# Recurrent scans over 32 images: statistics and row loads on ScalarE, the last drain in quarters

## The chip, the cores and the metric

The kernel runs on one core of a Trainium2 chip. The metric is the device time of one execution in microseconds (us). The engines are TensorE (PE; its weight loads are PEld), VectorE (DVE), ScalarE (ACT), GpSimd (POOL) and SyncE (SP). SP and ACT each own a queue from which transfers are issued.

## The reference

The input x has 32 images of 48 channels, 64 rows and 128 columns in float32. Two layers are alike: `x = x + scans(group_norm(x))`. The group norm uses 16 groups of 3 channels per image. Cut to what matters, one layer's scans are:

```python
def step(w, b):                       # 1-d convolution over 5 taps, 48 -> 48 channels
    return lambda carry, inp: inp + conv1d(carry, w, b)
D = scan(step(down_w, down_b), rows 0..63 of x)       # along a row, from row to row
U = scan(step(down_w, down_b), rows 63..0 of D)       # the end rows as D has them
R = scan(step(right_w, right_b), columns 0..127 of U) # along a column
L = scan(step(left_w, left_b), columns 127..0 of R)
```

Each step needs the one before it: 63 + 63 row steps and 127 + 127 column steps per layer and image.

## The kernel before, in words

A pass takes 8 images through one layer, so there are 8 passes: 0 to 3 for the four groups of images in layer 0, 4 to 7 in layer 1. (In names of the profile `row_12u` is layer 1, group 2, up: pass 6.) A pass has four stages:

- down and up: one `row_step` per row, nine matmuls (L323) with block weights `wd`, and three VectorE operations (L331) that add bias and input. The rows lie in the tile `arena` (view `rows`, 384 elements per row).
- `hand_over`: while up runs, finished rows are moved within `arena` to the layout for columns (view `cols`, which begins where row 20 ends). Twenty transfers (two row parities, ten pieces of channels) move 8 rows; the column steps need them all, column e of a row of eight needs the pieces of e.
- right and left: one `col_step` per column in two halves, six matmuls (L345 to L349) and two VectorE operations (L352).

Beside the stages runs side work, each a Python generator that the driving loop at the end of the program advances at chosen steps:

- `prepare` of the next group, in right: load x (L233, two transfers per tile of 4 rows), bn_stats on VectorE (L177), transpose on POOL (L243), store to the DRAM stage `xin` (L246).
- `drain` of the pass before, in down and up: `residual` loads the layer's input again (L283) and adds it on POOL. In layer 0 the sum goes into `arena` in place (L286), is stored to `mid`, and bn_stats on VectorE collect it for layer 1. In layer 1 it goes to the tile `perm` (L298) and out (L305). `cols` and `rows` share memory, so a row can be loaded for the next pass only when the chunks over it are drained.
- `fetch` loads rows from `xin` or `mid` (L257, nine or ten transfers per 8 rows on SP's queue) and normalises them in place with 24 ScalarE operations (L261). The first 20 rows are fetched in left, the others behind the chunks that free them.

After the last pass, its drain stands alone. At the start, group 0's preparation stands alone.

Instructions of an engine run in a written order, made from the program order by a scheduler of the framework. Semaphores order the engines. All transfers, of SP's and ACT's queue together, take eight completion semaphores (DMAHW0 to DMAHW7) in turn in the scheduled order, and a transfer waits for the one before it on its semaphore. A transfer behind a waiting one on its queue waits too.

Of the kernel before, what the change touches and what calls it, by code (L numbers as in the profile page):

```python
# [30 lines left out]
F32 = mybir.dt.float32  # L31
# [24 lines left out]
EARLY = 3  # L56

# [27 lines left out]
def kernel(  # L85
# [40 lines left out]
    maskp = const([P, NG, FULL], "maskp")  # L126
    last = const([FULL, ROW], "last")
# [13 lines left out]
    nc.gpsimd.memset(arena[32:64], 0.0)  # L141
    for t in nats + perms:
        nc.vector.memset(t[32:64], 0.0)
    nc.vector.memset(wd, 0.0)
    nc.scalar.dma_start(mask_sb, mask)
# [25 lines left out]
    def stat_tile(n, name, key):  # L171
        return stat_pool.tile([P, n], F32, tag=name, name=f"{name}_{key}")

    def collect(st, j: int, t, key: str):

        for b in range(GB):
            nc.vector.bn_stats(st[:, b, j, :], t[:, b])  # L177

    def scaling(st, key: str):

        mv = stat_tile(2 * GB, "mv", key).rearrange("p (b k) -> p b k", k=2)
        for b in range(GB):
            nc.vector.bn_aggr(mv[:, b], st[:, b].rearrange("p j k -> p (j k)"))
        ps = ps_stat.tile([FULL, NG + 1, 2 * GB], F32, tag="ps_stat", name=f"ps_{key}")
        nc.tensor.matmul(ps[0:P, NG, 0:GB], mask_sb, mv[:, :, 0], start=True, stop=True)
        pair = stat_tile(2 * GB, "pair", key)
        nc.vector.tensor_copy(pair[:, 0:GB], mv[:, :, 0])
        dev = stat_tile(GB, "dev", key)
        nc.vector.tensor_tensor(dev, mv[:, :, 0], ps[0:P, NG, 0:GB], ALU.subtract)
        sq = stat_tile(GB, "sq", key)  # L190
        nc.vector.tensor_tensor(sq, dev, dev, ALU.mult)
        nc.vector.tensor_tensor(pair[:, GB:], sq, mv[:, :, 1], ALU.add)
# [29 lines left out]

    def prepare(g: int):


        st = stat_pool.tile([P, GB, NCH, 6], F32, tag="st", name=f"st_x{g}", bufs=1)
        for j in range(NCH):
            nat, perm = nats[j % 2], perms[j % 2]
            h0 = 2 * CH * j
# [9 lines left out]
            collect(st, j, nat, f"x{g}_{j}")  # L239
# [10 lines left out]
        return scaling(st, f"x{g}")  # L250

    def fetch(layer: int, g: int, j: int, scale, offset):
# [3 lines left out]
        for e, c0, c1, o, p0 in PIECES:  # L256
            nc.sync.dma_start(rows[p0 : p0 + c1 - c0, hs, o], src[e][c0:c1])  # L257
# [11 lines left out]
    def hand_over(j: int):  # L269

        qs = slice(RB // 2 * j, RB // 2 * (j + 1))
        for r in range(2):
            src = rows[:, RB * j : RB * (j + 1)].rearrange("p (q r) o n -> r o p q n", r=2)
            dst = cols[SIDES[r], qs].rearrange("p q e k b -> e p q (k b)")
            for e, c0, c1, o, p0 in PIECES:
                nc.sync.dma_start(dst[e][c0:c1], src[r, o][p0 : p0 + c1 - c0])
# [84 lines left out]
    def drive(gen, key):  # L361

        coeffs[key] = yield from gen
# [126 lines left out]
```

## Time and profile before

| what | us |
|---|---|
| runs | 6104.42, 6104.59, 6112.84; median 6104.59 |
| profiled execution | 6102.24 |
| its span, first to last instruction | 6100.3 |
| granted TensorE clock | 0.919 of full speed |
| start, until the first row step | 182.5 |
| down / up / right / left, shortest seen | 136.7 / 127.2 / 172.7 / 170.2 |
| last drain, behind the last column step | 212.6 |

An engine's busy time is the sum of its instructions' durations. "Idle before" is how long it stood before instructions of a group, with what ended the wait. Stages are read by windows of time: the length of a window, what each engine was busy in it, and the clock that TensorE was granted.

### The profile page before, as it was taken

The numbers are of one execution on the slowest core, as the hardware profiler recorded it, in microseconds if no ns is written. First come the engines' busy times: TensorE is split into PE (matmuls) and PEld (weight loads), VectorE is DVE, ScalarE is ACT, GpSimd is POOL, SyncE is SP. The second block draws the span as 40 slices with busy tenths as digits, with TensorE's granted clock in tenths as the row PEclk, the third lists the DMA queues.
The fourth block names the chain that finished last, engine by engine and source line by source line (L and its number), as shares of the span: only waits on it lengthen the run. The fifth ranks groups of instructions, "written<-read, shape, count | busy, mean of one in ns | idle before, by whom it ended". The sixth has DMA issues, their size and how long they took to land. (4 is left out here: it accounts for less than half of the span.)

```text
span 6100.3 us, 102555 instructions
## 1 busy us (share of the span) xinstructions
PE 5016.6 (82%) x42592; PEld 4979.0 (82%) x42592; DVE 2870.0 (47%) x8277; ACT 843.3 (14%) x1737; POOL 1067.5 (17%) x333
## 2 busy tenths in 40 slices
PE   0799987889878898689987999779988699796960
PEld 0799987889878898689977999779988699796960
DVE  3446555555555555545555455334543255343530
ACT  0600222002220021202031200302022200400000
POOL 5103012120120201200022001420034000430025
PEclk9999998999989999899988999889999799898985
DMA  6636246552464533632065401642045500642014
GB/s 141 134 90 137 42 85 132 118 119 46 85 133 112 118 53 76 136 85 40 1 121 126 89 1 37 130 112 55 1 83 123 127 1 1 131 116 58 1 43 112
DMA packets 646130, 511.64 MB, mean 84 GB/s; under 512 B 55616, under 2 KB 596288, under 8 KB 645664
## 3 DMA queue, kind: packets, MB, share of 16 engines
q1 hardware_dynamic: 639680, 504.18, 38.6%
q8 instruction: 335, 5.49, 0.4%
q10 hardware_dynamic: 5984, 0.90, 0.1%
q14 instruction: 131, 1.07, 0.1%
HBM read 253.23 MB, written 150.99 MB: 66 GB/s over the span
## 5 line engine op out<-in xcount | busy, mean ns | idle before, releaser
L298 POOL TENSOR_TENSOR perm<-arena,nat 112x1024 f32<-112x1024 f32 x128 | 486.8, 3832 | 2304.1 <-DVE arena L352 1809.3
L261 ACT ACTIVATE arena<-arena,offset_m,scale_m 128x128 f32<-128x128 f32 (+1 forms) x864 | 420.6, 584 | 2203.6 <-DMA arena<-mid 1298.0
L286 POOL TENSOR_TENSOR arena<-arena,nat 112x2048 f32<-112x2048 f32 x64 | 288.7, 4529 | 1635.8 <-DVE arena L352 1072.6
L261 ACT ACTIVATE arena<-arena,offset_x,scale_x 128x128 f32<-128x128 f32 (+1 forms) x864 | 419.6, 583 | 771.9 <-DMA arena<-xin 730.6
L243 POOL COPY perm<-nat 112x1024 f32<-112x1024 f32 x128 | 254.3, 2021 | 904.6 <-DMA nat<-in_x 683.3
L177 DVE BATCH_NORM_STATS2 st_m<-arena 112x6 f32<-112x256 f32 x512 | 273.7, 605 | 17.7 <-POOL arena L286 17.7
L177 DVE BATCH_NORM_STATS2 st_x<-nat 112x6 f32<-112x256 f32 x512 | 179.7, 411 | 116.7 <-DMA nat<-in_x 113.8
L323 PE MATMUL row_10d<-arena,wd 128*128 128x128 f32 x1134 | 149.6, 300 | 44.4 <-DVE arena L331 39.1
L323 PE MATMUL row_02d<-arena,wd 128*128 128x128 f32 x1134 | 149.9, 300 | 44.0 <-DVE arena L331 38.9
L323 PE MATMUL row_03d<-arena,wd 128*128 128x128 f32 x1134 | 146.4, 295 | 47.4 <-DVE arena L331 43.8
L323 PEld LDWEIGHTS row_10d<-arena,wd 128*128 128x128 f32 x1134 | 146.2, 214 | 47.6 <-DVE arena L331 42.0
L323 PEld LDWEIGHTS row_02d<-arena,wd 128*128 128x128 f32 x1134 | 146.6, 215 | 47.2 <-DVE arena L331 41.8
L323 PE MATMUL row_01d<-arena,wd 128*128 128x128 f32 x1134 | 150.2, 301 | 41.8 <-DVE arena L331 37.6
L323 PEld LDWEIGHTS row_03d<-arena,wd 128*128 128x128 f32 x1134 | 142.4, 209 | 51.2 <-DVE arena L331 42.8
L323 PEld LDWEIGHTS row_01d<-arena,wd 128*128 128x128 f32 x1134 | 146.8, 215 | 45.0 <-DVE arena L331 40.5
L323 PE MATMUL row_11d<-arena,wd 128*128 128x128 f32 x1134 | 140.9, 290 | 39.5 <-DVE arena L331 39.5
L323 PE MATMUL row_12d<-arena,wd 128*128 128x128 f32 x1134 | 139.9, 289 | 39.9 <-DVE arena L331 28.2
L323 PEld LDWEIGHTS row_11d<-arena,wd 128*128 128x128 f32 x1134 | 138.4, 205 | 41.9 <-DVE arena L331 41.8
L323 PEld LDWEIGHTS row_12d<-arena,wd 128*128 128x128 f32 x1134 | 137.5, 204 | 42.2 <-DVE arena L331 42.2
L323 PE MATMUL row_13d<-arena,wd 128*128 128x128 f32 x1134 | 137.4, 286 | 40.3 <-DVE arena L331 28.1
L323 PEld LDWEIGHTS row_13d<-arena,wd 128*128 128x128 f32 x1134 | 135.1, 201 | 42.6 <-DVE arena L331 42.6
L323 PE MATMUL row_02u<-arena,wd 128*128 128x128 f32 x1134 | 143.3, 294 | 17.2 <-DVE arena L331 17.2
(199 smaller groups left out, 13052.8 us busy)
## 6 DMA issues: line engine op xcount, KB each, us to landing
arena<-arena SPq DMA_DIRECT2D x768, 96.0 KB, 2.3
nat<-in_x SPq DMA_DIRECT2D x128, 384.0 KB, 6.4
xin<-perm SPq DMA_DIRECT2D x128, 384.0 KB, 4.8
nat<-xin SPq DMA_DIRECT2D x128, 384.0 KB, 8.3
mid<-arena SPq DMA_DIRECT2D x128, 384.0 KB, 5.1
nat<-mid SPq DMA_DIRECT2D x128, 384.0 KB, 6.3
out<-perm SPq DMA_DIRECT2D x256, 192.0 KB, 2.7
arena<-xin SPq DMA_DIRECT2D x168, 192.0 KB, 5.6
```

The source lines that it names most:

```text
L177: nc.vector.bn_stats(st[:, b, j, :], t[:, b])
L243: nc.gpsimd.tensor_copy(perm5[:, r], nat[:, r])
L261: nc.scalar.activation(view[:, o, b], view[:, o, b], AF.Identity, bias=offset[:, o, b : b + 1], scale=scale[:, o, b : b + 1],)
L286: nc.gpsimd.tensor_tensor(res, res, nat, ALU.add)
L298: nc.gpsimd.tensor_tensor(perm[:, t].rearrange("p (b k e) -> p b k e", b=GB, k=NK), cols[:, q + t].rearrange("p e k b -> p b k e"), nat[:, ...
L323: nc.tensor.matmul(ps[o][:, a:b], wd[:, n], prev[:, i, a + s * GB : b + s * GB], start=seen[o] == 1, stop=seen[o] == left[o],)
```

## The change

The change has six parts.

1. Row loads of `fetch` are issued on ACT's queue (L352 in the changed program), just ahead of the 24 ScalarE operations that use them.
2. bn_stats on VectorE stay for group 0 alone. For the other groups `input_moments` loads x a second time in 16 halves of images, and `result_moments` loads `mid` again in 16 tiles. `collect` sums each tile on ScalarE with an accumulator (L195), POOL turns the sums into means (L199, L200), and a second ScalarE operation sums the squared deviations (L204). `scaling` joins the parts on VectorE.
3. In layer 0 the residual sum goes into the loaded tile `nat` (L382) instead of `arena`.
4. `drain` is advanced at every third step up to step 27. `input_moments` is advanced in down and up of the pass before the one it serves, `result_moments(0)` in those of pass 3, the others in right and left.
5. At the start, loads use free parts of `arena` as further staging tiles. The clear of `arena` is cut to 1536 elements and one clear per staging tile (L314), half of them on VectorE.
6. `hand_over` moves the last 8 rows in three parts (rows 4 to 7, 2 to 3, 0 to 1); their odd rows go on ACT's queue, 30 transfers per pass. The last pass is drained by `last_residual` in four parts of 32 columns, part 3 first, while left runs; part 0 stands behind the last step, with two thirds of its adds on VectorE and half of its stores on ACT's queue. The pieces in DRAM are 128 bytes.

```diff
-    nc.gpsimd.memset(arena[32:64], 0.0)
+    nc.gpsimd.memset(arena[32:64, H * ROW + 7 * CH * PAIR :], 0.0)
...
+    def collect(mo, t: int, views, key: str):
+        bs = slice(min(views), max(views) + 1)
+        for b, view in views.items():
+            nc.scalar.activation(
+                view, view, AF.Identity, scale=sides, accum_out=mo.mean[:, b, t : t + 1]
+            )
+        neg = stat_tile(GB, "neg", key)
+        nc.gpsimd.tensor_scalar(neg[:, bs], mo.mean[:, bs, t], -1.0 / mo.n, None, ALU.mult)
+        nc.gpsimd.tensor_scalar(
+            mo.mean[:, bs, t], mo.mean[:, bs, t], 1.0 / mo.n, None, ALU.mult
+        )
+        for b, view in views.items():
+            nc.scalar.activation(
+                view, view, AF.Square, bias=neg[:, b : b + 1],
+                accum_out=mo.dev2[:, b, t : t + 1],
+            )
...
+    def result_moments(g: int):
+        mo = Moments(NCH, W * CH, f"m{g}")
+        src = stages[1][g].rearrange("(q r) c n -> r c q n", r=2)
+        for j in range(NCH):
+            t = perms[j % 2]
+            for r in range(2):
+                nc.sync.dma_start(t[SIDES[r]], src[r, :, CH * j : CH * (j + 1)])
+            view = t.rearrange("p q (n b) -> p b (q n)", b=GB)
+            collect(mo, j, {b: view[:, b] for b in range(GB)}, f"m{g}_{j}")
+            yield
+        coeffs[1, g] = scaling(mo)
...
-            collect(st, j, nat, f"x{g}_{j}")
+            if first:
+                for b in range(GB):
+                    nc.vector.bn_stats(st[:, b, j, :], nat[:, b])
...
         for e, c0, c1, o, p0 in PIECES:
-            nc.sync.dma_start(rows[p0 : p0 + c1 - c0, hs, o], src[e][c0:c1])
+            nc.scalar.dma_start(rows[p0 : p0 + c1 - c0, hs, o], src[e][c0:c1])
...
-    def hand_over(j: int):
+    def hand_over(h0: int, h1: int):
         for r in range(2):
+            eng = nc.scalar if r and h1 <= RB else nc.sync
...
-                nc.sync.dma_start(dst[e][c0:c1], src[r, o][p0 : p0 + c1 - c0])
+                eng.dma_start(dst[e][c0:c1], src[r, o][p0 : p0 + c1 - c0])
...
-            nc.gpsimd.tensor_tensor(res, res, nat, ALU.add)
+            nc.gpsimd.tensor_tensor(nat, res, nat, ALU.add)
...
+    def last_residual(g: int, part: int):
+        kn = NK // 4
+        ks = slice(part * kn, (part + 1) * kn)
+        nq = 4 * CH
+        for i, q in enumerate(range(0, HP, nq)):
...
+            for t in range(nq):
+                for r in range(2):
+                    nc.sync.dma_start(nat[SIDES[r], t], ...)
+            for t in range(nq):
+                eng = nc.vector if part == 0 and t % 3 else nc.gpsimd
+                eng.tensor_tensor(perm[:, t], cols[:, q + t, :, ks], nat[:, t], ALU.add)
+                for r in range(2):
+                    dma = nc.scalar if part == 0 and r else nc.sync
+                    dma.dma_start(out[...], perm[SIDES[r], t])
+            yield
...
+            if h % RB == 0 and h:
+                hand_over(h, h + RB)
+            elif h in SPLITS:
+                hand_over(h, SPLITS[h])
...
+                if not nxt and i % 32 == 0:
+                    side["last"] = last_residual(g, i // 32)
+                if not nxt and i % 8 == 0:
+                    advance(side, "last")
```

(Views in `last_residual` are shortened here; `SPLITS = {4: 8, 2: 4, 0: 2}`.)

Three places show how the order of instructions moves. The first is POOL at the border from pass 0 to pass 1. Before, the transposes of x for group 1 are followed by the residual adds of pass 0's drain:

```order
L243 COPY perm_83<-nat_81 112x1024 x2
L243 COPY perm_82<-nat_80 112x1024 x2
L243 COPY perm_83<-nat_81 112x1024 x2
L286 ISA
L286 TENSOR_TENSOR arena<-arena,nat_80 112x2048
L286 TENSOR_TENSOR arena<-arena,nat_81 112x2048
```

After the change the means for group 2 (16 steps, two operations each, first and last shown) stand between the two:

```order
L331 COPY perm_84<-nat_82 112x1024 x2
L199 TENSOR_SCALAR neg_x_00_5779<-mean_x_5774 112x1
L200 TENSOR_SCALAR mean_x_5774<-mean_x_5774 112x1
...
L199 TENSOR_SCALAR neg_x_71_7844<-mean_x_5774 112x1
L200 TENSOR_SCALAR mean_x_5774<-mean_x_5774 112x1
L382 TENSOR_TENSOR nat_81<-arena,nat_81 112x2048
L382 TENSOR_TENSOR nat_82<-arena,nat_82 112x2048
```

ScalarE has the same there: its last sums for group 2 (L195, L204), then the row loads (L352) and their normalising operations (L356):

```order
L195 ACTIVATE perm_84,mean_x_5774<-perm_84,sides 112x2048
L204 ACTIVATE perm_84,dev_x_5775<-perm_84,neg_x_71_7844 112x2048
L352 DMA arena<-xin_86 48x8x128 x2
L352 DMA arena<-xin_86 32x8x128
L352 DMA arena<-xin_86 16x8x128
...
L356 ACTIVATE arena<-arena,offset_x_2744,scale_x_2742 128x8x16 x24
```

So the adds and the row loads of pass 1 stand behind all sums for group 2. The same holds in passes 2 and 3; in pass 3 it is 14 of the 16 sums of the first result.

The second place is the end of up in pass 1. Before, SP's last twenty pieces follow each other, each with the next semaphore:

```order
L276 DMA arena<-arena 48x4x128 [waits DMAHW5_49,DVE_49]
L276 DMA arena<-arena 48x4x128 [waits DMAHW6_49]
L276 DMA arena<-arena 32x4x128 [waits DMAHW7_49,PE_49]
L276 DMA arena<-arena 16x4x128 [waits DMAHW0_49,DVE_49]
L276 DMA arena<-arena 48x4x128 [waits DMAHW1_49]
```

After, these are SP's pieces of row 25 and its pairs (rows 25, 27, 29, 31) from the fourth on:

```order
L372 DMA arena<-arena 48x4x128 [waits DMAHW5_49]
L372 DMA arena<-arena 48x4x128 [waits DMAHW6_49]
L372 DMA arena<-arena 16x4x128 [waits DMAHW1_49]
L372 DMA arena<-arena 32x4x128 [waits DMAHW2_49]
L372 DMA arena<-arena 48x4x128 [waits DMAHW3_49]
```

and these are ACT's first pieces in that pass, of row 3 and of rows 5 and 7:

```order
L372 DMA arena<-arena 48x128 [waits DMAHW3_49,DMAHW2_49,DMAHW4_49,DVE_49,Activation_49]
L372 DMA arena<-arena 16x128 [waits DMAHW6_49,DMAHW5_49,Activation_49]
L372 DMA arena<-arena 32x128 [waits DMAHW7_49,DVE_49]
L372 DMA arena<-arena 32x2x128 [waits DMAHW2_49,DMAHW1_49,Activation_49]
```

In the scheduled order these stand among each other: SP's wait for DMAHW5 is for ACT's second piece here, those for DMAHW1 and DMAHW2 are for the pieces of rows 5 and 7. ACT's first piece waits for row 3 on VectorE (DVE). Behind the row-25 piece SP has 67 pieces up to and with the first of row 0.

The third place is the end of SP's queue. Before, the drain alternates loads of 4096-byte pieces and stores of 512-byte pieces:

```order
L283 DMA nat_80<-mid_91 48x2x1024
L305 DMA out<-perm_83 48x8x128 x4
L283 DMA nat_80<-mid_91 48x2x1024
L283 DMA nat_81<-mid_91 48x2x1024
L305 DMA out<-perm_82 48x8x128 x4
```

After, from the end of the last hand-over on:

```order
L416 DMA nat_81<-mid_92 48x8x32 x16
L416 DMA nat_82<-mid_92 48x8x32 x16
L432 DMA out<-perm_83 48x8x32 x16
L432 DMA out<-perm_84 48x8x32 x16
L416 DMA nat_81<-mid_92 48x8x32 x16
L432 DMA out<-perm_83 48x8x32 x16
```

Two chunks are loaded ahead; from the third on, 16 loads and 16 stores alternate, down to part 0, which has 8 stores per chunk on SP.

More of the change, by code (lines that the diff above doesn't have):

```diff
@@ L56 @@
 EARLY = 3
+SPLITS = {4: 8, 2: 4, 0: 2}
 PRODUCTS = (
@@ L171, in stat_tile @@
     def stat_tile(n, name, key):
[L172 to L183, printed above, removed]
+        bufs = 1 if n > 2 * GB else None
@@ L408 @@
     load_col_weights(0, nc.scalar)
-    for _ in drive(prepare(0), (0, 0)):
+    for _ in prepare(0):
         pass
```

195 lines of the change are left out of this document (148 added, 47 removed).

## The prediction

> **What bounds the kernel now.** I read the busy table first, then the busy time by stage, then the groups of instructions, and last the timeline of SP's queue at the places where TensorE stands still.
>
> ```profile
> span 6100.3 us, 102555 instructions
> PE 5016.6 (82%) x42592; PEld 4979.0 (82%) x42592; DVE 2870.0 (47%) x8277; ACT 843.3 (14%) x1737; POOL 1067.5 (17%) x333
> ```
>
> The recurrence on TensorE and VectorE is the bound, and it is 82% busy, so what can be won is where it waits. The windows are: the start, down and up of pass 0, the wait between up and right in pass 1, then down to the start of right for passes 1 to 4 and 5 to 7, the right stages of passes 0 to 3, the last left stage, the end. Behind the window stand its length, the engines' busy time, the granted clock, DMA share and GB/s.
>
> ```profile
> 0.00:182.50 182.50, 2.01 (x8) 1.81 (x8) 57.16 (x153) 4.81 (x11) 96.55 (x37) 1.00 0.66 148
> 182.50:319.20 136.70, 131.47 (x1135) 130.55 (x1136) 65.54 (x204) 101.23 (x208) 8.11 (x4) 1.00 0.64 116
> 319.20:446.40 127.20, 126.77 (x1136) 126.57 (x1134) 63.11 (x198) 0.00 (x0) 4.46 (x3) 1.00 0.38 92
> 1169.80:1178.30 8.50, 0.02 (x1) 0.05 (x1) 0.00 (x0) 0.00 (x0) 0.00 (x0) 0.70 0.49 120
> 814.10:1178.30 364.20, 289.61 (x2279) 284.87 (x2278) 192.25 (x527) 71.30 (x145) 72.69 (x17) 0.89 0.56 122
> 1575.60:1945.90 370.30, 294.30 (x2278) 289.55 (x2276) 192.60 (x527) 71.24 (x145) 72.59 (x17) 0.87 0.55 120
> 2345.20:2710.70 365.50, 285.50 (x2278) 280.15 (x2277) 192.20 (x527) 71.24 (x145) 72.61 (x17) 0.90 0.56 121
> 3053.70:3424.10 370.40, 293.73 (x2278) 288.97 (x2276) 192.61 (x527) 71.19 (x145) 72.63 (x17) 0.87 0.55 120
> 3767.10:4132.50 365.40, 267.47 (x2270) 264.91 (x2269) 122.61 (x379) 71.19 (x144) 123.58 (x33) 0.86 0.55 121
> 4474.60:4839.60 365.00, 266.55 (x2271) 264.03 (x2269) 122.44 (x379) 71.23 (x144) 123.40 (x33) 0.86 0.54 121
> 5183.00:5544.60 361.60, 264.06 (x2271) 261.61 (x2269) 122.35 (x379) 71.20 (x144) 123.55 (x33) 0.86 0.55 122
> 448.00:643.90 195.90, 180.27 (x1532) 177.51 (x1533) 124.97 (x377) 5.89 (x16) 51.99 (x26) 0.95 0.68 141
> 1178.30:1405.40 227.10, 194.19 (x1533) 191.08 (x1533) 132.82 (x401) 2.57 (x7) 63.81 (x32) 0.91 0.65 135
> 1945.90:2175.00 229.10, 195.92 (x1533) 192.84 (x1534) 132.78 (x401) 3.94 (x11) 63.85 (x32) 0.90 0.64 135
> 2710.70:2883.40 172.70, 172.68 (x1524) 172.70 (x1525) 88.72 (x253) 34.03 (x72) 0.00 (x0) 0.98 0.23 41
> 5716.90:5887.70 170.80, 170.41 (x1526) 170.21 (x1524) 89.43 (x255) 0.00 (x0) 0.00 (x0) 1.00 0.00 1
> 5887.70:6100.30 212.60, 0.00 (x0) 0.00 (x0) 0.00 (x0) 0.00 (x0) 117.75 (x32) 0.51 0.46 111
> ```
>
> Undisturbed, down takes 136.7, up 127.2, right 172.7, left 170.8. Right in passes 0 to 2 is 23, 54 and 56 longer, and VectorE is busy there for 36 to 44 us more. Down, up and the wait before right take 364 to 370 in passes 1 to 4 where pass 0 needs 265.5. The granted clock is 1.00 where nothing waits and 0.86 to 0.90 in the disturbed stretches; I let it come back with the waits gone. 395 us at the two ends have no recurrence at all.
>
> ```profile
> L177 DVE BATCH_NORM_STATS2 st_m<-arena 112x6 f32<-112x256 f32 x512 | 273.7, 605 | 17.7 <-POOL arena L286 17.7
> L177 DVE BATCH_NORM_STATS2 st_x<-nat 112x6 f32<-112x256 f32 x512 | 179.7, 411 | 116.7 <-DMA nat<-in_x 113.8 <-DMA maskp<-in_mask 2.8
> L261 ACT ACTIVATE arena<-arena,offset_x,scale_x 128x128 f32<-128x128 f32 x672 | 343.9, 608 | 717.0 <-DMA arena<-xin 687.0 <-DVE arena L331 30.0
> L261 ACT ACTIVATE arena<-arena,offset_x,scale_x 128x64 f32<-128x64 f32 x192 | 76.3, 494 | 54.9 <-DMA arena<-xin 43.6 <-DVE offset_x L220 11.3
> L298 POOL TENSOR_TENSOR perm<-arena,nat 112x1024 f32<-112x1024 f32 x128 | 486.8, 3832 | 2304.1 <-DVE arena L352 1809.3 <-DMA nat<-mid 354.4 <-issue 121.4
> ```
>
> **The statistics.** 896 of the 1024 bn_stats leave VectorE: per group 128 x 0.605 = 77 us in the down and up behind it, 128 x 0.411 = 53 us in right. In right nothing else is added, so passes 0 to 2 return to 172.5: 652.1 - 517.5 = **-135**. What replaces them is ScalarE's work on reloaded data. One normalising operation takes 343.9/672 = 0.51 us for 128 elements and 76.3/192 = 0.40 for 64, so by these two rows 0.28 and 1.8 ns per element: a 256-element sum is 0.74 and a result step of 16 such takes 12, an input step, two of 2048, at most 8. No row of this case shows an accumulator. With the hand to POOL and back I count 16 x 9 = 144 us for an input group and 16 x 12.5 = 200 for a result group. In the new order both stand ahead of the residual adds and the row loads on ScalarE, POOL and SP. They run in right and left, 342 us, behind the preparation of x, eight pairs of tiles at the pace of the start:
>
> ```profile
> 94.42 7.82 POOL L243 COPY perm<-nat 112x1024 f32<-112x1024 f32 x4 [9.86 <-DMA nat<-in_x]
> 111.68 7.81 POOL L243 COPY perm<-nat 112x1024 f32<-112x1024 f32 x4 [9.44 <-DMA nat<-in_x]
> ```
>
> 111.7 - 94.4 = 17.3 a pair, 140 in all, some 10 behind right's start. 150 + 144 = 294 is covered with 48 to spare. For the first result group, 150 + 200 = 350 is not quite, though its last two steps stand later: I put 10 us on pass 3, between 0 and 40. The reloads lie there too, and so does their traffic. Each group's scaling gains some ten small operations on VectorE, 0.4 us each at most by the row of L177; it is busy for 89 of 171 us in left, so I count nothing, and 8 x 4 = 32 if none were hidden.
>
> **Down and up, passes 1 to 4.** Row loads now need no turn on SP. A load is 9 or 10 issues on ScalarE's queue, about 6 us in which it computes nothing, some 2 to land, and 24 operations x 0.51 = 12.3: 20.5 us. Six stand behind each other from about 11 us on, so the rows from 60 on are ready at 134, where TensorE alone would be there at 60 x 2.17 = 130. The residual's sum goes to its own tile, so its rows are free at the add's end and not after store and bn_stats; that is in the 20.5 too. Down becomes 143 and up, free of bn_stats, 126.5. Between 136.7 and 160 is open.
>
> **The hand-over.** SP's issues in a row by the timeline (start, length, count), what one takes to land by the DMA table, and the spread of single issues (ns, least/median/most). T is the end of up, T0 the start of down.
>
> ```profile
> 4083.69 3.29 SPq L276 DMA_DIRECT2D arena<-arena  x5
> arena<-arena SPq DMA_DIRECT2D x768, 96.0 KB, 2.3
> arena<-mid SPq DMA_DIRECT2D x168, 192.0 KB, 5.1
> 4012.14 4.67 SPq L305 DMA_DIRECT2D out<-perm  x4
> 4026.31 4.66 SPq L305 DMA_DIRECT2D out<-perm  x4
> 3809.30 5.98 SPq L257 DMA_DIRECT2D arena<-mid  x9
> 3828.12 0.84 SPq L305 DMA_DIRECT2D out<-perm  x2
> L305 SPq DMA_DIRECT2D out<-perm x256: 315/392/1626, 3771.6 to 6096.5; - x128
> L257 SPq DMA_DIRECT2D arena<-mid x360: 302/450/1773, 2746.0 to 5345.1; - x180
> ```
>
> One piece costs 3.29/5 = 0.66 us of SP. Each transfer waits for the one eight before it in the common order, on whichever queue that is. Before, all were SP's, and with its 20 last pieces SP is past the end of up by 8.5. Now 30 odd-row pieces stand on ScalarE's queue, and the first of them waits for row 3, which is done three steps of 127.2/63 = 2.02 before the end of up, T - 6. But by the order SP's pieces of row 25 take the semaphore behind just these, so SP, whose rows 25 to 8 have long been finished, stands until T - 6 + 2.3 = T - 4. From there to the first piece of row 0 it issues 67 pieces: 67 x 0.66 = 44, which lands at **T + 42**. In passes 3 and 4 row loads stand among them, and three that SP waits for take 5.1 - 2.3 = 2.8 more: T + 50; in pass 0 reloads of x do the like, and I take 50 too. Without this coupling, SP has 50 left at the end and right starts at about T + 10. Passes 1 and 2: 143 + 126.5 + 42.5 = 312 against 364.2 and 370.3, -52 and -58; pass 3 321 + 10 = 331, -34; pass 4 321, -49: together **-193**. Pass 0 loses: 137 + 127 + 50, with 3 for issues between the normalising steps, 317 against 265.5, **+51**.
>
> **Passes 5 to 7.** What is late here is SP itself: the chunks' stores come 4026.3 - 4012.1 = 14.2 apart where no row load stands between; where one does, it takes about 6 us of SP. Before, the last ended at 4031, T0 + 264. Without row loads 16 chunks from T0 + 10 end at T0 + 223, and then 166 pieces x 0.66 = 110 and some 12 of waits on loads follow: right starts at T0 + 345, and at 336 in pass 7 with no loads. Against 365.4, 365.0 and 361.6 that is **-65**, and it may be nothing to -90.
>
> **The start.**
>
> ```profile
> 0.74 33.80 POOL L141 MEMSET arena<- 32x40448 f32 x1 [0.29 <-POOLq L480]
> 24.68 24.83 ACTq L159 DMA_DIRECT2D wd<-in_w  x43
> 34.59 7.79 POOL L243 COPY perm<-nat 112x1024 f32<-112x1024 f32 x4
> 47.76 4.87 SPq L233 DMA_DIRECT2D nat<-in_x  x4
> ```
>
> The clear of 33.8 falls to about 13 of 2048-element pieces, so the first pair of copies could end 20 us sooner. But the stores behind it now stand in the common order among ScalarE's 70 weight loads, which run to 49.5, and the second pair waits for those. The loads still stand behind the stores of the pair before, so later pairs keep their pace of 17.3, with row loads between them. I take **0**, between -20 and +10.
>
> **The end.** 212.6 us of drain become quarters of the columns. By the order, SP holds for every 8 rows 16 loads and then 16 stores of 384 packets each: 16 x 0.66 (row L257: 5.98/9) + 8 x 0.84 = 17.3 us, where the program plans 8 column steps, 10.7. Part 3 may begin 31 of 127 steps into left, at 41; its first two chunks are loaded by then and go at POOL's pace, 16 adds of 3.83/4, to 57. Ten chunks x 17.3 end at 230, part 0 with half its stores on ScalarE needs 4 x 14 = 56, and 2.7 to land: 289, less 171 of left, 118 instead of 212.6: **-94**. With the issue medians, 0.45 and 0.39, it would be 71; with 0.66 for every issue 162.
>
> **Sum.** -135 - 193 + 51 - 65 + 0 - 94 = -436 on the span of 6100.3; the profiled execution took 6102.2, the median of the runs is 6104.6. 5666, say **5670**.
>
> **Rivals.** The third needs the price of a packet: the DMA queue over 13.2 us of hand-over, 4083.6 to 4096.8 (packets, MB, share of 16 engines).
>
> ```profile
> q1 hardware_dynamic: 3401, 1.58, 49.1%
> ```
>
> 1. *Sums are dear.* If an accumulating operation costs ScalarE twice a plain one, a result step is 24 us and a group 384: pass 3 waits until 150 + 384 - 342 = 192 into its down, three later groups 42 each, input groups (16 x 16 = 256) 64 twice and 40 in pass 0. 486 more is 6155, slower than before; at 1.5 times it is pass 3 with about 100, 5770. The sign turns near 1.9. Against it: nothing in the long rows of L261 hints at it; for it: each also hands a sum to POOL and waits.
> 2. *The queues do not couple* at the hand-over: gaps of 10 in five passes, -170: 5500. Against it stands the order, which lists ScalarE's pieces ahead.
> 3. *Small stores are dear.* In those 13.2 us 3401 packets of 512 bytes took 16 x 13.2 x 0.491 / 3401 = 30.5 ns each. At twice that, a store of 384 on 16 engines takes 1.46 us instead of 0.42: chunks of 34 us, tail 355, 5905. At the row's own price the 24 packets per engine take 0.73 us, little above the issue, and the sum stands. The Trainium skill speaks for this rival: "DMA: Bandwidth & Descriptors", Specifications, gives 512 bytes as the smallest piece at line rate and a read-modify-write below it, and these stores are pieces of 128. By that rule it would be 5905 and not 5670; no run here shows such a store.
> 4. *SP keeps up at the end* with the medians: 5625.
>
> **Chances.** As summed, with down and start inside their bounds (5590 to 5760), 0.52; rival 2 0.12; rival 4 0.08; rival 3 0.10; rival 1 at 1.5 times 0.10, at 1.9 or more 0.06; the rest 0.02. Leaving out rival 3, rival 1's worst and the rest, 0.18 in all, gives 5500 to 5890. Faster by over 0.2%, which is about what these runs can tell, 0.92; the same 0.02; slower 0.06.
>
> **What would show it.** Right in passes 0 to 2 near 172.5, no bn_stats behind the start. A wait of 40 to 50 us before every right stage from pass 0 to 4, ended by a transfer of SP, with SP idle shortly before the end of up: this decides most. POOL's residual adds starting with their down and not behind the moments. SP issuing without a pause through the last left stage. The prediction fails if ScalarE's sums reach into down by tens of us, or if SP's wait for row 3 is not there.

## The result, and the profile after

The changed kernel takes 5953.58 us (median of 4 runs, 5951.03 to 5961.04) against 6107.94 for the kernel before (4 runs, 6104.42 to 6112.84): a ratio of 0.9749 [0.9732, 0.9766]. It is faster, by about a third of what was forecast: 154 us instead of 435, and outside the range (5500 to 5890). The profiled execution took 5961.04, its granted clock was 0.922.

The busy table first, then the windows that answer to those of before: the start, the wait before right in pass 0, down to right in passes 1, 3 and 5, right in pass 1, then left of pass 3, right of pass 4 and left of pass 5, and the end.

```profile
span 5959.3 us, 105466 instructions
PE 4860.6 (82%) x42592; PEld 4846.2 (81%) x42592; DVE 2548.1 (43%) x7387; ACT 1812.3 (30%) x3977; POOL 1087.5 (18%) x640
```

```profile
0.00:229.70 229.70, 2.05 (x9) 1.85 (x9) 70.38 (x167) 4.84 (x11) 76.78 (x44) 1.00 0.85 165
495.20:550.70 55.50, 2.02 (x9) 1.82 (x9) 4.33 (x16) 4.41 (x5) 4.35 (x4) 0.54 0.48 100
894.30:1212.40 318.10, 258.96 (x2278) 258.20 (x2277) 130.57 (x393) 71.67 (x145) 72.70 (x17) 0.91 0.65 140
2215.70:2545.70 330.00, 264.58 (x2278) 262.62 (x2276) 124.64 (x395) 109.55 (x247) 74.26 (x23) 0.90 0.67 147
3677.20:4025.30 348.10, 265.70 (x2278) 263.11 (x2276) 137.28 (x393) 71.67 (x145) 120.62 (x33) 0.88 0.63 135
1212.40:1384.30 171.90, 171.88 (x1524) 171.90 (x1525) 88.77 (x253) 34.38 (x72) 63.81 (x32) 0.99 0.84 167
2718.30:2958.90 240.60, 173.40 (x1529) 173.21 (x1527) 89.41 (x256) 74.82 (x202) 2.87 (x12) 0.86 0.13 24
3280.50:3506.80 226.30, 175.34 (x1524) 175.14 (x1525) 89.06 (x255) 200.65 (x520) 6.70 (x28) 0.87 0.39 67
4197.10:4429.50 232.40, 173.19 (x1529) 173.00 (x1527) 89.39 (x256) 65.59 (x165) 1.91 (x8) 0.87 0.07 13
5810.80:5959.30 148.50, 0.00 (x0) 0.00 (x0) 12.53 (x21) 0.00 (x0) 50.80 (x48) 0.51 0.60 92
```

VectorE lost 322 us of work and ScalarE gained 969, yet TensorE's share stayed at 82%. The seventh to ninth windows are the surprise: three stages that took 170 to 173 us before now take 226 to 241, with TensorE no busier in them. Set out by place, all from such windows of the two traces (us):

| place | before | forecast | after | after minus forecast |
|---|---|---|---|---|
| start | 182.5 | 182.5 | 229.7 | +47 |
| pass 0, down to right | 265.5 | 317 | 321 | +4 |
| right of passes 0 to 2 | 652.1 | 517 | 518 | +1 |
| passes 1 to 4, down to right | 1470.4 | 1277 | 1287.5 | +10 |
| left of 3, right of 4, left of 5 | 513 | 513 | 699.3 | +186 |
| passes 5 to 7, down to right | 1092 | 1027 | 1043.3 | +16 |
| end | 212.6 | 118 | 148.5 | +30 |

But for rounding, the last column adds up to the whole miss of 295 us of the span (5959.3 against 5664). What ended the long stages is told by the waits of the stretch 2718 to 2960 (engine, tile, line, what it waited for; total, times, longest), and by the same row over the whole trace:

```profile
DVE total_m L219 <- POOL mean_m L200: 67.3, 1, 67.3
PE col_03l L476 <- DVE arena L483: 67.2, 1, 67.2
...
DVE total_m L219 <- POOL mean_m L200: 177.8, 3, 67.3
```

One VectorE instruction, the reduction of the means (L219), waits 67.3 us for POOL, and TensorE waits 67.2 for VectorE's column step, which stands behind it. It happens three times, for 67.3, 51.1 and 59.4 us: 178 of the 186 us. VectorE's written order shows why. These are consecutive rows of it:

```
L483 SCALAR_TENSOR_TENSOR arena<-col_03l_20557,bc,arena 112x32x4
L483 SCALAR_TENSOR_TENSOR arena<-col_03l_20562,bc,arena 112x32x4
L219 TENSOR_REDUCE total_m_22084<-mean_m_19252 112x8
L220 TENSOR_SCALAR pair_m_22083<-total_m_22084 112x8
L483 SCALAR_TENSOR_TENSOR arena<-col_03l_20567,bc,arena 112x32x4
```

The reduction stands behind the fifth operation of left. On the timelines POOL computes the last of the 16 means at 2789.24 (L200), and VectorE goes on at once:

```profile
2776.72 0.23 POOL L199 TENSOR_SCALAR neg_m<-mean_m 112x8 f32<-112x8 f32 x1 [11.63 <-ACT perm L195]
2788.92 0.23 POOL L199 TENSOR_SCALAR neg_m<-mean_m 112x8 f32<-112x8 f32 x1 [11.63 <-ACT perm L195]
2789.24 0.24 POOL L200 TENSOR_SCALAR mean_m<-mean_m 112x8 f32<-112x8 f32 x1
2789.51 0.29 DVE L219 TENSOR_REDUCE total_m<-mean_m 112x8 f32<-112x128 f32 x1 [67.35 <-POOL mean_m L200]
```

In the other two stages the reduction stands behind operation 231 of right and behind the first of left. Why the scheduler put it there no run shows.

The start has its own waits. These are SP's, in the first 232 us, and POOL's copies near its end:

```profile
SPq L319 <- DMA arena<-xin: 43.7, 15, 5.0
SPq L334 <- DMA arena<-xin: 25.9, 10, 4.7
181.56 7.83 POOL L331 COPY perm<-arena 112x1024 f32<-112x1024 f32 x4 [17.73 <-DMA arena<-in_x]
208.30 3.94 POOL L331 COPY perm<-arena 112x1024 f32<-112x1024 f32 x2 [18.91 <-DMA arena<-xin]
```

SP's loads and stores of x wait 70 us in all for row loads (`arena<-xin`), which are on ACT's queue. No data goes from a row load to a load or store of x; what they share is the turn of the semaphores. The last pairs come 26.7 us apart, where before it was 17.3.

### The profile page after: what moved, and what is told of

Same layout as the page of the kernel before. It is cut to its first block, busy times and chain, and to the rows that moved or that the text cites. A ratio compares the mean times of both kernels' runs of the same rounds, so it can differ in the third digit from the quotient of the medians.

```text
span 5959.3 us, 105466 instructions
## 1 busy us (share of the span) xinstructions
PE 4860.6 (82%) x42592; PEld 4846.2 (81%) x42592; DVE 2548.1 (43%) x7387; ACT 1812.3 (30%) x3977; POOL 1087.5 (18%) x640
## 5 line engine op out<-in xcount | busy, mean ns | idle before, releaser
L356 ACT ACTIVATE arena<-arena,offset_m,scale_m 128x128 f32<-128x128 f32 (+1 forms) x864 | 425.6, 584 | 1243.6 <-DMA arena<-mid 895.1
L356 ACT ACTIVATE arena<-arena,offset_x,scale_x 128x128 f32<-128x128 f32 (+1 forms) x864 | 422.4, 590 | 901.2 <-DMA arena<-xin 738.6
L195 ACT ACTIVATE perm<-perm,sides 112x256 f32<-112x256 f32 (+1 forms) x560 | 476.2, 858 | 577.1 <-DMA perm<-in_x 192.4
L388 POOL TENSOR_TENSOR perm<-arena,nat 112x1024 f32<-112x1024 f32 x96 | 360.8, 3785 | 1154.8 <-DVE arena L483 459.7
L382 POOL TENSOR_TENSOR nat<-arena,nat 112x2048 f32<-112x2048 f32 x64 | 289.2, 4533 | 671.5 <-DMA nat<-xin 353.9
L204 ACT ACTIVATE perm<-perm,neg_m 112x256 f32<-112x256 f32 x512 | 381.0, 752 | 13.7 <-POOL neg_m L199 13.7
L331 POOL COPY perm<-nat 112x1024 f32<-112x1024 f32 x100 | 200.0, 2034 | 646.7 <-DMA nat<-in_x 599.8
L199 POOL TENSOR_SCALAR neg_m<-mean_m 112x8 f32<-112x8 f32 x64 | 15.1, 236 | 1250.1 <-ACT perm L195 1250.1
L424 POOL TENSOR_TENSOR perm<-arena,nat 112x256 f32<-112x256 f32 x108 | 114.4, 1067 | 485.4 <-DVE arena L483 328.1
L476 PE MATMUL col_10r<-arena,wc 112*112 112x128 f32 x508 | 106.3, 292 | 97.3 <-DVE arena L483 50.9
L476 PE MATMUL col_03l<-arena,wc 112*112 112x128 f32 x508 | 105.5, 290 | 67.2 <-DVE arena L483 67.2
L476 PE MATMUL col_11l<-arena,wc 112*112 112x128 f32 x508 | 105.4, 290 | 59.2 <-DVE arena L483 59.2
L454 PE MATMUL row_03d<-arena,wd 128*128 128x128 f32 x1134 | 137.1, 286 | 18.2 <-DVE arena L462 18.2
```

Of the source, the lines that this page charges most:

```text
L195: nc.scalar.activation(view, view, AF.Identity, scale=sides, accum_out=mo.mean[:, b, t : t + 1])
L204: nc.scalar.activation(view, view, AF.Square, bias=neg[:, b : b + 1], accum_out=mo.dev2[:, b, t : t + 1],)
L331: nc.gpsimd.tensor_copy(perm5[:, r], nat[:, r])
L356: nc.scalar.activation(view[:, o, b], view[:, o, b], AF.Identity, bias=offset[:, o, b : b + 1], scale=scale[:, o, b : b + 1],)
L382: nc.gpsimd.tensor_tensor(nat, res, nat, ALU.add)
L388: nc.gpsimd.tensor_tensor(perm[:, t].rearrange("p (b k e) -> p b k e", b=GB, k=NK), cols[:, q + t].rearrange("p e k b -> p b k e"), nat[:, ...
```

## The experiments

Twelve kernels, in the order of the questions. Beside them ran the kernel before, at 6111.66 us (e1 to e4), 6099.67 (e5 to e8), 6101.47 (e9 to e11) and 6100.45 (e12). A time without a ratio is that of a single run. The kernel before ranges from 6094 to 6114 us beside them, so a difference of ten us or so between two kernels says nothing.

The code below is cut to the lines that matter.

**1. The reductions in VectorE's queue.** e1 adds the 16 means pairwise on POOL, so that VectorE has no instruction left that needs them early.

```diff
-            nc.vector.tensor_reduce(total, mo.mean, mybir.AxisListType.X, ALU.add)
-            nc.vector.tensor_scalar(pair[:, 0:GB], total, 1.0 / T, None, ALU.mult)
+            part, half, at = mo.mean, T // 2, 0
+            while half:
+                dst = dev[:, :, at : at + half]
+                nc.gpsimd.tensor_tensor(dst, part[:, :, :half], part[:, :, half : 2 * half], ALU.add)
+                part, at, half = dst, at + half, half // 2
+            nc.gpsimd.tensor_scalar(pair[:, 0:GB], part[:, :, 0], 1.0 / T, None, ALU.mult)
```

> The reduction of a group's means (L219, L220), which stands in VectorE's order among the column steps, goes to POOL as pairwise adds; nothing else changes. Theory: these three waits of VectorE for the last sum (67, 51 and 59 us) are the whole excess of the three long column stages, so they return to 171 to 173 us and the kernel gains about 185, to 5770. Rival: the sums themselves are late, whoever needs them; then the wait turns up at the matmul behind the left stage or at the row loads, and the gain is under 60.

5772.69 us (5771.05 to 5773.46), ratio 0.9448 [0.9434, 0.9463]: 181 less than the changed kernel. The three stages, by windows of e1:

```profile
2720.10:2890.50 170.40, 170.40 (x1529) 170.40 (x1527) 89.05 (x254) 75.89 (x204) 4.10 (x17) 1.00 0.18 34
3210.20:3382.30 172.10, 172.09 (x1524) 172.09 (x1525) 88.69 (x253) 159.29 (x417) 5.58 (x24) 0.99 0.46 79
4075.20:4245.60 170.40, 170.40 (x1529) 170.40 (x1528) 89.03 (x254) 64.50 (x161) 3.14 (x13) 1.00 0.08 15
```

ScalarE's sums are all still there, and no stage is long. So the loss needs the consumer in VectorE's queue; the sums alone do not cause it.

e11 goes at the same wait from the other side. It keeps the reductions on VectorE and leaves out the second ScalarE sum (L204) of the results, half of the work that is waited for; the deviations are set to a constant instead.

```diff
-        for b, view in views.items():
+        for b, view in views.items() if mo.T < NCH else ():
             nc.scalar.activation(view, view, AF.Square, ...)
```

> The changed kernel without the squared sums of the four result groups (8 of 16 operations per step are left out, the deviations are a constant), the reductions still on VectorE; by the order they stand 33 column steps, 45 us, earlier among the column steps. Theory: the waits of VectorE are the lateness of ScalarE's last sum against the place of the reduction. A group of sums takes 99 us less and the place is 45 earlier, so each of the three long stages loses about 54 us and is at 172 to 190; pass 3's down loses its 10: about 5790. Rival: the wait comes from the reloads of mid or from POOL's small operations, which are unchanged; then the stages stay above 210.

5838.13 us. The stalls shrink but stay; by the waits of e11:

```profile
DVE total_m L219 <- POOL mean_m L200: 63.9, 3, 24.7
```

63.9 instead of 177.8, and all three waits now lie in right, which takes 191, 199 and 200 us in passes 3 to 5, where 172 to 190 was expected. The expectation had the reductions 45 us earlier. On the timelines they stand 69, 77 and 83 column operations earlier, at 0.67 us each 46, 52 and 56 us. That is part of the difference; the rest stays open. In both kernels the reductions stand ahead of the moment when ScalarE is done.

**2. The start.** e2 puts pass 0's row loads back on SP; all others stay on ACT's queue.

```diff
-        fetch(0, 0, j, *coeffs[0, 0])
+        fetch(0, 0, j, *coeffs[0, 0], nc.sync)
```

(`fetch` takes the queue as an argument for this.)

> Only the row loads of pass 0 go back to SP's queue. Theory: the start is longer because these row loads share the eight semaphores with the loads and stores of x while both run; without them the start falls from 230 to about 180 us, and the kernel to about 5905. Rival: the weight loads on ScalarE's queue hold the second pair and everything behind it; then the start stays above 215.

5907.72 us, 46 less. The start is 182.1, SP has no wait for `arena<-xin` left, and the copies come 18.2 apart:

```profile
126.33 7.83 POOL L331 COPY perm<-arena 112x1024 f32<-112x1024 f32 x4 [10.35 <-DMA arena<-in_x]
144.55 7.83 POOL L331 COPY perm<-arena 112x1024 f32<-112x1024 f32 x4 [10.40 <-DMA arena<-in_x]
```

Then why is the start no shorter than before, with 20 us less of clearing? e7 (built on e5, below) was to hand out the weights' loads one by one between the loads of x.

```diff
-    load_row_weights(0, nc.scalar)
+    weights = load_row_weights(0, nc.scalar)        # now a generator
...
+        for _ in range(7):
+            next(weights, None)
```

> As the run with the four repairs, but the 78 row weight loads of the start are spread over the first 12 tiles of x, seven per tile. Theory: the 20 us that the shorter clear of the arena should bring were taken by the weight loads, which stand in one block before the second pair; spread out they delay no pair, and the start falls from 182 to 160 to 170. Rival: spread out they delay each pair a little, and the start stays at 180 or grows.

5523.05 us, start 181.3, as in e5 (179.9): but the scheduler issued the weights as early as ever, and the second pair of copies still began at 45.7 and 52.8. The edit did not make the case, so this run tells nothing. e10 does: e6 (below) with no loads of layer 0's row weights at all, zeros in their place.

```diff
-    load_row_weights(0, nc.scalar)
```

> As the fastest kernel, but the 78 row weight loads of layer 0 are left out, so its passes compute with zero weights; the work of all engines is the same in time. Theory: these loads hold the stores of the first pair and the loads of the second through the shared semaphores and eat the 20 us of the shorter clear; without them the start falls from 182 to 160 to 165. Rival: the second pair waits for its own loads; then the start stays above 178.

5363.29 us, start 161.5, against 182.2 in e6. In e6 the second pair of copies began at 46.1 and 53.6, and SP's loads and stores of x waited 31 us for the weights; in e10 the pair waits for its own load of x alone. First SP's waits of e6 up to 90 us, then the first of the pair in e10:

```profile
SPq L339 <- DMA wd<-in_w: 16.7, 6, 5.9
SPq L324 <- DMA wd<-in_w: 14.7, 6, 5.3
33.78 3.95 POOL L336 COPY perm<-arena 112x1024 f32<-112x1024 f32 x2 [10.29 <-DMA arena<-in_x]
```

So the weights' loads cost 20.7 us of the start, as much as the shorter clear was to bring. How long the start of the kernel before would be without them was not run. In the whole kernel only 8 of the 20.7 show, a difference too small for one run to tell; down of pass 4 took 149.4 there and 139.5 in e6, and why stays open.

**3. The hand-over.** e3 moves the last 8 rows in one part again, all on SP.

```diff
-SPLITS = {4: 8, 2: 4, 0: 2}
+SPLITS = {0: 8}
-            eng = nc.scalar if r and h1 <= RB else nc.sync
+            eng = nc.sync
```

> All pieces of the hand-over on SP's queue, the last 8 rows in one part as before, 160 pieces per pass. Theory: SP's wait for row 3 goes; the wait before right falls from 45 to 55 us to about 9 in passes 0 to 4 (4 times 36 and once 46) and, with 40 pieces fewer but 30 back on SP, by 10 to 20 in passes 5 to 7: 5954 - 190 - 45 = about 5720. Rival: the row loads on ScalarE's queue couple SP all the same in passes 3 to 6, then the waits of passes 3 and 4 stay at 25 or more, and the kernel at 5770.

5780.14 us (5766.61 to 5784.2), ratio 0.9454 [0.9438, 0.9469], 173 less. The waits before right in passes 0 to 4 fall from 55.5, 44.8, 44.6, 46.9 and 46.0 to 16.5, 14.2, 13.8, 29.2 and 20.5; in passes 5 to 7 only from 48 to 52 to 38 to 44. In pass 3 SP also waits 12 us for ACT's row loads, by its waits at the end of up:

```profile
SPq L372 <- DMA arena<-mid: 12.0, 3, 10.4
```

In the program the pieces stand ahead of these loads and need nothing of them, so this looks like the same coupling with another partner; no run shows it alone.

In the changed kernel itself, the rows for pass 1 are SP's wait for ACT's pieces, and ACT's pieces on the timeline:

```profile
SPq L372 <- DMA arena<-arena: 28.4, 9, 24.3
...
1161.05 26.09 ACTq L372 DMA_DIRECT2D arena<-arena  x30
```

Up ends at 1167.7; ACT's pieces begin 6.6 ahead of that (the prediction: T - 6), and SP stands 24.3 us with rows ready. The Trainium skill, "DMA: Bandwidth & Descriptors", Anatomy of one DMA, a section on transfers that GpSimd issues, says that DMA engines do not wait on semaphores and that any such wait is spent on the sequencer that issues. The trace agrees: those 24.3 us are SP's, and all that is behind it on the queue is late with it.

Then e6, with the repairs of e1, e2 and e4 (below), puts the odd rows of every block on ACT's queue, not of the last only.

```diff
-SPLITS = {4: 8, 2: 4, 0: 2}
+SPLITS = {0: 8}
-            eng = nc.scalar if r and h1 <= RB else nc.sync
+            eng = nc.scalar if r else nc.sync
```

> As the run with the four repairs, but the odd rows of every block of the hand-over stand on ScalarE's queue, none ahead of its turn. Theory: in passes 5 to 7 SP is late by its own issues (160 pieces behind the drain), half of them take 53 us less, so the wait before right there falls from 44 to 10 or less and the kernel gains 90 to 110 on the four repairs, to about 5415; the waits of passes 0 to 4 stay below 20. Rival: any two queues that share the semaphores couple; then the waits of passes 0 to 4 return to 30 or more and the kernel is slower than with the four repairs.

5371.24 us (5362.54 to 5378.27), ratio **0.88** [0.8781, 0.8819], the fastest of the kernels that compute everything. It gains 154 us on e5 (below), where 90 to 110 was expected, as the waits of passes 0 to 4 fell too. The waits are 12.2, 4.3, 3.0, 5.8, 3.5, 16.0, 13.0 and 13.5. Down to right in pass 1, and SP's waits for other pieces while it hands over in that pass:

```profile
804.20:1083.60 279.40, 262.13 (x2278) 260.98 (x2278) 125.32 (x393) 71.63 (x145) 80.62 (x21) 0.96 0.81 167
SPq L377 <- DMA arena<-arena: 16.5, 9, 3.6
```

Pieces of the same rows become ready together on both queues. SP still waits for pieces, but 3.6 us at most with its own (7.7 with a store of the drain), where it was 24.3, and each queue has half of the pieces to issue. e3 and e6 also move the last 8 rows in one part again; a run with one of these edits alone is missing.

**4. The end.** e4 puts half of the stores of all four parts on ACT's queue.

```diff
-                    dma = nc.scalar if part == 0 and r else nc.sync
+                    dma = nc.scalar if r else nc.sync
```

> Odd-row stores of the last drain on ScalarE's queue in all four parts, not only in part 0. Theory: the end is bound by SP's issues, 19.6 us per chunk of 16 loads and 16 stores; with 8 stores fewer on SP a chunk takes 15 to 15.5, ten chunks gain 40 to 45, and the end falls from 148 to about 105. Rival: the small packets bind (DMA engines or the order of landing), then the chunk stays above 18 and the end above 135.

5919.94 us, the end 111.9 instead of 148.4. Of SP's timeline, first the changed kernel behind the last step and then e4:

```profile
5831.57 8.27 SPq L432 DMA_DIRECT2D out<-perm  x16
5839.89 10.44 SPq L416 DMA_DIRECT2D nat<-mid  x16
```

```profile
5849.83 4.98 SPq L432 DMA_DIRECT2D out<-perm  x8
5854.86 10.45 SPq L416 DMA_DIRECT2D nat<-mid  x16
```

SP issues without a pause in both: the end is bound by issuing.

**5. All repairs.** e5 is e1, e2, e3 and e4 together.

> The four changes of the first four runs together: totals on POOL, first rows on SP, hand-over on SP in blocks of 8 rows, half of all last stores on ScalarE. Theory: they act in different places, so their gains add up: 181 + 46 + 174 + 37 from 5954 gives 5515. Rival: a shorter wait before right leaves ScalarE's sums less time, so pass 3's down grows and the sum is missed by 40 or more.

5525.46 us (5518.54 to 5531.55), ratio 0.9054 [0.9039, 0.907]. The four alone gave 181, 46, 173 and 34, 434 in all; together they give 428. So they are four separate losses.

**6. What each part is worth.** e8 puts all row loads of the changed kernel back on SP.

```diff
-            nc.scalar.dma_start(rows[p0 : p0 + c1 - c0, hs, o], src[e][c0:c1])
+            nc.sync.dma_start(rows[p0 : p0 + c1 - c0, hs, o], src[e][c0:c1])
```

> The changed kernel with all row loads back on SP's queue and nothing else changed. Theory: in passes 5 to 7 the 54 loads, 6 us for each 9, stand again between the chunks, so the drain ends 40 us later and the wait before right grows by 30 to 40 each; in passes 1 to 4 down gets 5 to 20 longer; the start falls to 182 as in the run with the first rows on SP. Sum 5954 - 47 + 110 + 40 = 6055. Rival: the place of the row loads does not matter once bn_stats are gone, and only the start changes: 5907.

6039.27 us. That is near the expected 6055, by another road. The down stages of passes 1 to 4 are 143 to 146, no longer than with the loads on ACT's queue (146 to 155); those of passes 5 to 7 are 181 instead of 170, and most waits grow (pass 3: 71.3, passes 5 to 7: 67 to 69). So ACT's queue pays where SP is the late one, and does nothing for the down stages of passes 1 to 4. What did shorten those?

e9 puts bn_stats back on VectorE, on the base of e6; no sums on ScalarE.

```diff
-            if first:
-                for b in range(GB):
-                    nc.vector.bn_stats(st[:, b, j, :], nat[:, b])
+            for b in range(GB):
+                nc.vector.bn_stats(st[:, b, j, :], nat[:, b])
```

(and the same in `residual` behind the add; `input_moments` and `result_moments` go.)

> The fastest kernel so far (odd hand-over rows on ScalarE) with bn_stats on VectorE for all groups again, for x in right and for the result behind the residual add; no reloads and no sums on ScalarE. Theory: on VectorE the statistics cost what the profile before showed: right in passes 0 to 2 grows by 24 to 57, up of passes 1 to 4 by 37 to 41, down by 20 to 40: 5371 + 136 + 156 + 110 = about 5775. So moving them is worth about 400 us, of which the changed kernel gave 182 back at the three reductions. Rival: with row loads and hand-over off SP's path VectorE has room for them, and it stays below 5500.

5634.34 us (5629.4 to 5643.26), ratio 0.9229 [0.9213, 0.9244]: moving the statistics is worth 263 us here. Down and right of pass 1 in e9 (up takes 158.4):

```profile
803.20:990.70 187.50, 151.81 (x1136) 149.38 (x1135) 109.46 (x285) 71.65 (x144) 54.32 (x12) 0.86 0.69 146
1155.80:1342.30 186.50, 178.28 (x1533) 176.09 (x1533) 122.91 (x373) 6.26 (x17) 48.17 (x25) 0.97 0.72 147
```

Down is long again with the row loads still on ACT's queue, but right only by 14 (172.1 in e6), where before it was 54. Was the forecast for right true by chance? e12 asks the kernel before: the same, with bn_stats of one tile of sixteen for all but group 0.

```diff
+            if g == 0 or j == 0:
+                collect(st, j, nat, f"x{g}_{j}")
-            collect(st, j, nat, f"x{g}_{j}")
```

(and the same for the results.)

> The kernel before, with bn_stats of one tile of sixteen instead of all for groups 1 to 3 of x and for the four results (the scale and offset are then wrong); everything else is as before. It parts what the statistics themselves cost on VectorE from what else the change did in the same stages. Prediction's reading: all that right of passes 0 to 2 is longer than 172.7 (23, 54 and 56) is bn_stats, and so is all that up of passes 1 to 4 is longer than 127.2 (155 together): right 172 to 175 in each, up 127 to 130, down of passes 1 to 4 still near 190 because SP sets it; about 5815 in all. Rival, from the run with bn_stats put back (only 10, 14 and 15 came back in the rights): bn_stats are worth a quarter to a third there and the rest comes from the loads of x and the transposes behind SP; right stays at 185 to 210, and the time at about 5950.

5733.42 us, 220 less than the whole change, with SP's queue as it was. Down, up, the wait and right of pass 1 in e12:

```profile
797.20:942.50 145.30, 133.62 (x1145) 132.68 (x1144) 68.97 (x217) 71.35 (x145) 45.21 (x10) 0.94 0.76 167
942.50:1069.70 127.20, 126.77 (x1136) 126.58 (x1134) 60.89 (x190) 0.00 (x0) 27.49 (x7) 1.00 0.54 129
1069.70:1100.40 30.70, 0.00 (x0) 0.00 (x0) 0.00 (x0) 0.00 (x0) 0.00 (x0) 0.56 0.50 121
1100.40:1277.20 176.80, 174.78 (x1533) 174.55 (x1534) 94.32 (x281) 6.60 (x18) 63.67 (x32) 0.98 0.81 173
```

Right of passes 0 to 2 is 172.3, 176.7 and 176.2, so there the prediction's reading of before was right. Down is 145 to 147 in passes 1 to 4, which neither reading expected: it was bn_stats, not row loads waiting their turn on SP. TensorE's waits for VectorE in down of pass 1 say the same. They are long in the kernel before and in e9, which have bn_stats, and short in e8 (10.9 us) and e12 (9.0), which have their row loads on SP. First before, then e9:

```profile
PE row_01d L323 <- DVE arena L331: 37.6, 14, 3.7
PE row_01d L463 <- DVE arena L471: 35.7, 12, 7.0
```

Over the kernel, e12's down gives 188, up 155 and right 127; 99 come back as longer waits for SP's pieces (30.7 in pass 1 against 8.5); 371 remain, of a span that is 369 shorter.

Why bn_stats cost right so much less in e9 than in the kernel before can be read from VectorE's timelines of pass 1's right. Before, 120 of its 128 bn_stats stand in blocks of eight, and a column step behind a block waits for all of it. In e9, 96 fall into this stage; 24 of them stand in blocks of eight and 55 alone, in the gap between two column steps. A bn_stats group and TensorE's waits for VectorE, first before and then e9:

```profile
1245.92 2.70 DVE L177 BATCH_NORM_STATS2 st_x<-nat 112x6 f32<-112x256 f32 x8
1236.18 0.42 DVE L338 BATCH_NORM_STATS2 st_x<-nat 112x6 f32<-112x256 f32 x1
PE col_01r L345 <- DVE arena L352: 27.6, 15, 2.1
PE col_01r L485 <- DVE arena L492: 8.1, 7, 2.0
```

So the place of bn_stats in the written order counts and not only their time. No run changes the place alone.

## Why the prediction was wrong, point by point

- **"Each group's scaling ... I count nothing, and 8 x 4 = 32 if none were hidden": the step that failed**, 186 of the 295 us. It priced the durations of these operations and took VectorE's idle half as cover. A reduction lasts 0.29 us; what counts is that it holds up the column steps behind it in VectorE's order until ScalarE's sixteenth sum is handed over. This is shown by e1 (all of it comes back) and e11 (a good third is left when half of the work goes). Rival 1 named long sums as the way to a loss, but had them reach into the next down, by fetches. The price of a sum was as forecast: in the rows below (of the changed kernel's groups), a sum takes 0.75 us against the prediction's 0.74, with 0.19 for reading the accumulator, and the steps on POOL's timeline come 12.2 us apart against 12.5.

```profile
L195 ACT ACTIVATE perm<-perm,sides 112x256 f32<-112x256 f32 x512 | 380.2, 751 | 258.8 <-POOL nat L382 168.9 <-DMA perm<-mid 89.9
L195 ACT ACTIVATION_READ_ACCUMULATOR perm<-perm,sides 112x1 f32 x560 | 106.5, 190 | 0.0
```

- **The start, 0 forecast and +47 measured.** "later pairs keep their pace of 17.3, with row loads between them" is the step that failed: the rule of the eight semaphores that the prediction used at the hand-over holds here too, and the row loads, which wait for SP's stores of their rows, stand between SP's transfers (e2, -46). That the second pair waits for the weights' loads was forecast, and e10 shows it.
- **The end, 118 forecast and 148.5 measured: mis-sized.** A chunk took 18.9 to 20.9 us to issue, and ten of them 195.7, where the sum has 17.3 and 173: that is 23 of the 30 us, and the first chunks and part 0 were 4 later each. The term that was too small is the store: 16 of them took 8.3 to 9.4 us against 6.7, while 16 loads took 10.4 to 11.6 against 10.6. That issuing is the bound is shown by e4; rival 4 falls. So does rival 3, which needed 61 ns for a packet of a store: ACT's queue carried nothing but these stores from 5831 to 5956, and by the row below a packet took 16 x 125 x 0.081 / 12497 = 13 ns. The stores land in 1.9 us (median). The Trainium skill, "DMA: Bandwidth & Descriptors", Specifications, has a read-modify-write below 512 bytes; pieces of 128 cost nothing here that shows. The rows are of the DMA queue in that window and of the view of line L432:

```profile
q10 hardware_dynamic: 12497, 1.54, 8.1%
DMA to landing us min/median/max: 1.8/1.9/4.0
```

- **The hand-over was right** to 3 us where it was derived (44.8 and 44.6 against 42); where 50 was taken it was 55.5 in pass 0, 46.9 and 46.0. Rival 2 falls. The 50 of pass 4 is near by luck, since SP's pieces waited there 0.9 us for row loads and not the 8 that were added for them. e3 shows the size of the loss. e6 shows that two queues need not cost this: with half of every block on the second the waits are 3 to 6 us in passes 1 to 4.
- **Down in passes 1 to 4: the number right, the reason wrong.** 146, 146, 155 and 148 against 143, with 10 for pass 3. The prediction laid it to the row loads' turn on SP; e8 and e12 have the loads on SP and down at 143 to 147. It was bn_stats, as in up, so the number came out by luck. Of the 9.5 us above the undisturbed 136.7 in passes 1 and 2, the greater part is again a consumer of the new statistics, this time in TensorE's order: a matmul of the scaling waits 8.0 and 7.0 us for VectorE. This is the row of pass 1:

```profile
PE ps_x L241 <- DVE pair_x L237: 8.0, 1, 8.0
```

- **Right of passes 0 to 2** (518 against 517), up (127.2 against 126.5) and pass 0 (321 against 317) came as summed. In passes 5 to 7 it was 348.1, 348.6 and 346.6 against 345, 345 and 336, so the term of -65 was -49; pass 7 was to be 9 shorter for having no row loads and was 2, and why stays open.
- **Slips in the working, none of which decides.** 143 + 126.5 + 50 is 319.5 and not 321. With the issue medians the end comes to 65 and not 71. The 486 of rival 1 counts the 10 us of pass 3 twice. The traces list 62 row weight loads, where the prediction has 70 and the expectations of e7 and e10 have 78. A row load was given "some 2" us to land, though the prediction's own row has 5.1 for 192 KB; in the changed kernel it is 4.6 to 7.5.

So the expected gain is there: taking nearly all bn_stats off VectorE is worth 369 us of span in the kernel before (e12). The changed kernel left 434 us at four places, which single edits give back: VectorE's reductions (181), the hand-over (173), the start (46) and issuing at the end (34).

## What to carry to other kernels

When work moves from one engine to another, look for the instruction that consumes its result: if that stands in the written order of the bound engine, its cost is the wait and not its duration, and that order shows the place before any run. Two queues that take completion semaphores in one common turn hold each other up where their transfers become ready at different times; share out transfers that become ready together, not the last few. Before laying a long stage to one of two causes that both left it, take one away alone.

## What the runs showed of the hardware

A ScalarE sum of 256 elements takes 0.75 us here, and a separate read of its accumulator 0.19. A store of 48 KB in pieces of 128 bytes lands in 1.9 us; of the hand-over's pieces, in 512 bytes, those of 48 KB on SP land in 2.0. In a run without pauses an issue costs SP 0.52 us for a store (8.27/16) and 0.65 for a load (10.44/16); at the end of this kernel that sets the pace. A bn_stats of 0.42 us fits between two column steps, and eight in a row, 2.70 us, do not.
